# A graph sweep on one core: additions of counts without a wait for each other, and the loads of their places moved

## The chip, the cores and the metric

The kernel runs on 1 core of one Trainium2 chip. A core has a matrix engine (TensorE, PE in the profile; PEld is its loading of weights), a vector engine (VectorE, DVE), a scalar engine (ScalarE, ACT), GpSimd (POOL) and SyncE (SP). Each has an instruction queue of its own and waits for others by semaphores; SP, ACT and POOL also issue DMAs. The metric is the device time of one execution in microseconds (us): the median of 3 runs.

## The reference

A graph layer, batch norm and residual layer norm over N = 6250 nodes with D = 256 features and NE = 200000 edges, sorted by their target `dst`:

```
deg_out, deg_in = clip(segment_sum(1, src), 1), clip(segment_sum(1, dst), 1)
h = feats * rsqrt(deg_out)[:, None]
m = segment_sum(h[src], dst) * rsqrt(deg_in)[:, None]
x = m @ W_gc + b_gc + feats @ W_res + b_res
y = x + moe_ff(x)          # 64 experts, top 2, 256 -> 512 -> 256, gelu
out = layernorm(feats + batchnorm(y))
```

The targets are `6250 * u**2` with u uniform, so low nodes have many edges and high nodes few. The change lies in the stage that makes `segment_sum(h[src], dst)`, called the sweep here.

## The kernel before, in words

Ahead of the sweep (up to about 190 us) the degrees are counted and `h` is made, in SBUF (`hrow`) and in DRAM (`h_dram`). Behind it come routing, the experts and the two norms.

The edges stand in 1563 groups of 128 in order of their targets. The first 1118 groups are *dense*: for a window of 128 target nodes (a *column* c of 30), the kernel makes the matrix of counts (how many edges go from source s to window node t) and multiplies it with all of `hrow`. A column is cut into n *parts* of k groups, each part covering w neighbouring window nodes (`DENSE[c]` is g0, k, w, n). Part by part:

- DVE makes one-hots: `lo_of` (L684, through the helper at L287) the low digit of the source for 8 groups at a time, `hot_of` (L690) the high digit together with the target for a batch of groups.
- PE multiplies the two for each group (L712) into one of 5 PSUM banks `pc`: 49 x w counts in each of 128 partitions.
- ACT copies all but the part's first node to its place in `counts[c % 2]` (L729, L732), at a column that is read from a register.
- DVE adds the part's first node there (L749, 128 x 49), since that node can also be the last one of the part in front. The addition is made one part late (`carried`, L745). It frees the bank.

The places come from the table `places`: every eighth part a `TENSOR_LOAD` (L716) brings eight numbers into registers of ACT and DVE, at the point where the part's copy is written. Every addition was made to wait for the addition before it on the same engine, because two of them could touch the same column.

`multiply(c, t)` (L755) then takes the finished counts, 49 steps of two matmuls (L758, L759). The sweep's order is written out by hand in `dense` (L879): while column c is multiplied, column c + 1 is counted, so the additions of column 5 lie beside the multiplication of column 4. The remaining 445 groups are gathered: POOL fetches 128 rows of `h_dram` for one group by an indirect DMA (L626) into a ring of 8 blocks `r`, and PE multiplies each with a one-hot made on DVE (L631, L632, L935). These are put between the rest at equal distances of estimated time, and a block's next fetch is issued behind its last use. `x_step` puts small pieces of the next stage in between.

A check on the data (`off_parts`, L422, on the rises of nodes from part to part, given in `part`) sends everything to a slow general path when a part's nodes do not fit in its w.

Of the kernel before, what the change touches and what calls it, by code (L numbers as in the profile page):

```python
# [9 lines left out]
F32 = mybir.dt.float32  # L10
# [6 lines left out]
ALU = mybir.AluOpType  # L17
# [3 lines left out]
DVE_E = mybir.EngineType.DVE  # L21
SP_E = mybir.EngineType.SP
PE_E = mybir.EngineType.PE
ACT_E = mybir.EngineType.Activation

N = 6250
# [11 lines left out]
NE = 200000  # L38
NGR = 1568
NGU = -(-NE // 128)  # L40
WIN = 128
# [7 lines left out]
PAIRS = 8  # L49
# [36 lines left out]
def _node(g):  # L86

    return N * min(1.0, g * 128 / NE) ** 2
# [54 lines left out]
DENSE, GATHER, DENSE_PE = _plan()  # L143
GD = GATHER[0][0]
ND = len(DENSE)
# [6 lines left out]

BELOW = [max(0, int(_node(c[0]) - MARGIN) // TP) for c in DENSE]
ABOVE = [NT] + [-(-int(_node(c[0]) + WIN + MARGIN) // TP) for c in GATHER[:-1]]
LOW = [b * TP for b in BELOW] + [0] * len(GATHER)
# [4 lines left out]
def gnn_moe_kernel(ctx, tc, x_in, x_cols, src, dst, bases, nexts, firsts, parts, lasts, W_gc, b_gc, W_res, b_res, Wg, bg, w1, b1, w2, b2,  # L162
                   gamma, beta, out):
    nc = tc.nc
    V, S, G, T = nc.vector, nc.scalar, nc.gpsimd, nc.tensor
# [81 lines left out]
    with tc.tile_pool(name="edges", bufs=1) as ep, ExitStack() as later:  # L247
        iota_h = ep.tile([128, NS * WMAX, 2], FP16, name="iota_h")
        for a in range(0, NS * WMAX, 128):
            b = min(a + 128, NS * WMAX)  # L250
            V.tensor_scalar(iota_h[:, a:b, :], iota_f[:, :b - a, None].to_broadcast([128, b - a, 2]), float(a), None,
                            op0=ALU.add)
# [9 lines left out]
        places = ep.tile([ND, NPM], I32, name="places")  # L262
# [9 lines left out]
        for c, (g0, k, w, n) in enumerate(DENSE):  # L272
            a = g0
            while a < g0 + k * n:
# [4 lines left out]
                a = b  # L279
# [20 lines left out]
        with tc.tile_pool(name="late", bufs=1) as lp, tc.tile_pool(name="both", bufs=2) as bp, \  # L300
# [24 lines left out]
            part = dp.tile([128, 2, ND], F32, name="part")  # L325
# [19 lines left out]
            a, wides = 0, []  # L345
            for c, (g0, k, w, n) in enumerate(DENSE):
                if c == ND - 1 or DENSE[c + 1][2] != w:
# [3 lines left out]
                    a = c + 1  # L351
            S.activation(rows_w[:, 1, :], rows_w[:, 0, :], AF.Copy, scale=-1.0, bias=float(WIN - 1))
            pos = dp.tile([128, ND], F32, name="pos")
            away = dp.tile([128, 3, ND], F32, name="away")
# [8 lines left out]
            for k, values in enumerate((LOW, HIGH)):  # L363
                c = 0
# [36 lines left out]
            stepf = dp.tile([1, ND], F32, name="stepf")  # L401
            risen = dp.tile([ND, NPM], F32, name="risen")
            G.memset(stepf, 0.0)

            def windows():

# [14 lines left out]

            def off_parts():  # L422
                V.tensor_tensor(away[:, 0, :], part[:, 1, :], rows_w[:, 0, :], ALU.is_gt)
                V.tensor_scalar(away[:, 1, :], part[:, 1, :], 0.0, None, op0=ALU.is_lt)
                V.tensor_add(away[:, 0, :], away[:, 0, :], away[:, 1, :])

            def off_windows():
# [78 lines left out]
            for i in range(NGR // CG):  # L506
# [32 lines left out]
                for c in range(CG):  # L539
                    r = c % 2  # L540
# [3 lines left out]
                    else:  # L544
                        T.matmul(stp[64 * r:64 * r + 64, :], hot_row[:, c // 2, :, r], stairs[:, c - CV, :],
                                 start=(i == 0 and c < CV + 2), stop=(c0 + c >= NGR - 2))
# [13 lines left out]
                if i % 6 == 0 and 6 <= i <= 42:  # L560
                    r = i // 6 * 7
# [44 lines left out]
        with tc.tile_pool(name="xs", bufs=1) as xs, tc.tile_pool(name="hotg", bufs=2) as hg, \  # L606
# [12 lines left out]
            for i in range(NR):  # L619
                r = rp.tile([128, 2 * D + 2], F32R, name=f"r{i}")  # L620
# [25 lines left out]
            live = {"carry": []}  # L646
# [37 lines left out]
            def lo_of(q):  # L684

                if q * PAIRS < GD:
                    los[q] = hc.tile([128, PAIRS // 2, 128, 2], BF16, name="lo")
                    hot_pairs(los[q], lo_b, q * PAIRS, PAIRS, 128)

            def hot_of(q):  # L690
# [10 lines left out]
                for g in range(a, b):  # L701
                    hots[g] = hot[:, (g - e) // 2, :, (g - e) % 2]

            def count(g):

                c, j, i = groups[g]
                g0, k, w, n = DENSE[c]
                if i == 0:
                    live["pc"] = ps_c.tile([128, 512], F32, name="pc")
                r = g % PAIRS  # L710
                pc = live["pc"][:, :NS * w]
                T.matmul(pc, los[g // PAIRS][:, r // 2, :, r % 2], hots.pop(g), start=(i == 0),  # L712
                         stop=(i == k - 1))
                if i == k - 1:
                    if j % 8 == 0:
                        _, live["at"] = nc.values_load_multi_w_load_instructions(  # L716
                            places[c:c + 1, j:j + 8], engines=(ACT_E, DVE_E), min_val=0, max_val=WIN - w,
                            skip_runtime_bounds_check_because="clipped to what the window leaves")
                    carried(1)
                    at, pc = live["at"][j % 8], pc.rearrange("p (t w) -> p t w", w=w)  # L720
                    if j == 0:
                        live["adds"], live["carry"], live["puts"] = [], [], []
                    if c == 0 and j == 0:
                        live["puts"].append(S.copy(counts[0][:, :, :w], pc).ins)
                    else:
                        if j == 0:
                            step = nc.values_load(step_i[0:1, c:c + 1], engines=(DVE_E,), min_val=0, max_val=WIN - 1,
                                                  skip_runtime_bounds_check_because="clipped to the window")
                            put = S.copy(counts[c % 2][:, :, 1:w], pc[:, :, 1:])  # L729
                            to, had = counts[c % 2][:, :, 0:1], counts[(c - 1) % 2][:, :, ds(step, 1)]  # L730
                        else:
                            put = S.copy(counts[c % 2][:, :, 1:][:, :, ds(at, w - 1)], pc[:, :, 1:])  # L732
                            to = had = counts[c % 2][:, :, ds(at, 1)]
                        for a in live["adds"]:
                            tc.declare_no_dep(put.ins, a, reason="other columns of the window")
                        live["carry"].append((to, pc[:, :, 0:1], had, j))
                        live["puts"].append(put.ins)
                if g % PAIRS == 1:
                    lo_of(g // PAIRS + 1)
                if g == cuts[cut_of[g]][1] - 1:  # L740
                    hot_of(cut_of[g] + KB)
                if i == k - 1 and j == n - 1:
                    carried(0)

            def carried(but):  # L745

                while len(live["carry"]) > but:
                    to, more, had, j = live["carry"].pop(0)
                    add = V.tensor_tensor(to, more, f32(had), ALU.add).ins  # L749
                    tc.add_manual_dep(add, live["puts"][j].name, SYNCED, reason="its bank, and the column of the part in front")  # L750
                    for a in live["puts"][j + 1:]:
                        tc.declare_no_dep(add, a, reason="columns behind it")
                    live["adds"].append(add)

            def multiply(c, t):  # L755
# [212 lines left out]
            now, n = 0.0, 0  # L968
# [6 lines left out]
            for n in range(n, len(rows)):  # L975
# [6 lines left out]
                                    skip_runtime_bounds_check_because="a flag")  # L982
# [3 lines left out]
                                      skip_runtime_bounds_check_because="all groups or none")  # L986
            with tc.For_i(0, n_groups, 1) as gi:
# [10 lines left out]
                                       op0=ALU.mult, op1=ALU.add)  # L998
# [6 lines left out]
                for k in range(2):  # L1005
# [11 lines left out]
                start = ge.tile([128, 1], F32, name="start")  # L1017
                V.tensor_copy(start, low[:, 0:1])
                n_win = nc.values_load(numi, min_val=0, max_val=N // WIN + 1,
                                       skip_runtime_bounds_check_because="counted from the node numbers")  # L1020
                with tc.For_i(0, n_win, 1):
                    at = ge.tile([128, 1], F32, name="at")
# [45 lines left out]
    order = rpool.tile([1, E], I32, name="order")  # L1068
# [55 lines left out]
    with tc.tile_pool(name="xw", bufs=1) as xw, tc.tile_pool(name="xl", bufs=3) as xl, \  # L1124
# [42 lines left out]
        with tc.manual_schedule():  # L1167
            sums = {}
            for t0 in range(ta, tb, 2):
                n = min(2, tb - t0)  # L1170
# [9 lines left out]
            for t0, z in sums.items():  # L1180
                n = min(2, tb - t0)
# [4 lines left out]
                for t in range(t0, t0 + n):  # L1186
                    V.scalar_tensor_tensor(x[:, t, :], z[:, t - t0, :D], s_in[:, t - t0:t - t0 + 1], x[:, t, :],
                                           op0=ALU.mult, op1=ALU.add)
# [20 lines left out]
            for a, b in ((0, ta), (tb, NT)):  # L1209
                for t0 in range(a, b, 10):  # L1210
                    n = min(10, b - t0)
# [245 lines left out]
    with tc.tile_pool(name="ex", bufs=2) as xp, \  # L1457
# [202 lines left out]
        with tc.manual_schedule(engines={PE_E, ACT_E, DVE_E, SP_E}):  # L1660
# [6 lines left out]
                                skip_runtime_bounds_check_because="a flag")  # L1667
        with tc.For_i(0, n_left, 1), tc.tile_pool(name="all", bufs=1) as ap:
            V.memset(y_sum, 0.0)
            with tc.For_i(0, E, 1) as r:  # L1670
# [14 lines left out]
                with tc.For_i(0, FULL, 1) as i:  # L1685
                    idc = xp.tile([128, 1], I32, name="idc")
                    V.tensor_copy(idc, ids8[:, ds(i, 1)])
                    to = xp.tile([128, 1], I32, name="toc")
# [9 lines left out]
    with tc.tile_pool(name="fin", bufs=1) as fp, tc.tile_pool(name="gat", bufs=4) as gp, \  # L1698
# [71 lines left out]
        part = {}  # L1770
# [114 lines left out]
```

## Time and profile before

| | us |
|---|---|
| runs | 1501.49, 1506.61, 1509.82 (median 1506.61) |
| profiled execution | 1507.11 |
| its span | 1505.1 |
| granted TensorE clock, mean | 0.959 |
| sweep, first and last multiplication | about 190 to 905 |

In the profile a row of the engines' table is busy time, share and count of instructions. In rows of a group, "x" is the count, then come busy time, mean ns of one, the idle time of the engine ahead of them and what ended it. A row of waits has total us, times and the longest. A row of the timeline has start, duration, engine and line; "x2" means that two are merged, from the start of the first to the end of the second. Instructions of one engine overlap at their ends.

### The profile page before, as it was taken

What the parts mean: (1) busy time and instruction counts of PE and PEld (TensorE: products, weight loads), DVE (VectorE), ACT (ScalarE), POOL (GpSimd) and SP (SyncE); (2) the same over time, 40 slices, a digit from 0 to 9 for tenths busy, and PEclk for the clock granted to TensorE, in tenths of its full rate; (3) what the DMA queues carried; (4) which work ended last, traced back from release to release, by engine and by line L of the source; (5) the groups of instructions that cost most, each with busy time, mean ns of one, the idle gap of its engine ahead of it and who ended that gap; (6) DMA issues with size and microseconds to landing.
All of it is one profiled execution on the core that took longest, in us unless ns stands there. A gap on an engine that the chain in (4) does not pass through costs nothing. (4 is left out here: it accounts for less than half of the span.)

```text
span 1505.1 us, 33098 instructions
## 1 busy us (share of the span) xinstructions
PE 1347.8 (90%) x9805; PEld 1127.7 (75%) x9805; DVE 1127.2 (75%) x3325; ACT 763.2 (51%) x1966; POOL 797.9 (53%) x897
## 2 busy tenths in 40 slices
PE   5999478988999999999999994699999999999783
PEld 3555266877888899999999993588788888788441
DVE  8999889988888888888777746745555655444587
ACT  4676544456666666665555533433343333333358
POOL 6000215777776677776666635256666667565100
PEclk8999789999999999999999996899999999999888
DMA  5899665778777778787777755669777788687645
GB/s 180 264 283 323 240 241 155 197 220 236 201 221 221 220 214 232 210 221 211 222 203 217 214 156 192 125 196 295 229 247 253 253 251 268 206 250 246 236 142 155
DMA packets 211234, 332.81 MB, mean 221 GB/s; under 512 B 27989, under 2 KB 142814, under 8 KB 211045
## 3 DMA queue, kind: packets, MB, share of 16 engines
q1 hardware_dynamic: 156035, 176.48, 37.5%
q0 software_dynamic: 47888, 146.88, 34.4%
q10 hardware_dynamic: 7122, 7.26, 1.7%
q8 instruction: 79, 1.29, 0.4%
q14 instruction: 110, 0.90, 0.2%
HBM read 250.92 MB, written 73.15 MB: 215 GB/s over the span
## 5 line engine op out<-in xcount | busy, mean ns | idle before, releaser
L626 POOL DMA_INDIRECT r<-h_dram,srcg x445 | 469.8, 1056 | 243.3 <-PE pc L712 80.2
L758 PE MATMUL sm<-hrow,counts 128*128 128x258 f32 x1470 | 487.0, 346 | 8.8 <-DVE counts L749 8.7
L732 ACT CAST counts<-pc 128x196 f32 (+7 forms) x879 | 356.9, 406 | 211.1 <-PE pc L712 175.4
L759 PE MATMUL sm<-hrow,counts 128*128 128x256 f32 x1470 | 394.5, 282 | 0.0
L712 PE MATMUL pc<-hotk,lo 128*128 128x245 bf16 (+7 forms) x1118 | 304.7, 304 | 42.5 <-DVE counts L749 20.3
L758 PEld LDWEIGHTS sm<-hrow,counts 128*128 128x128 f32 x1470 | 286.6, 195 | 27.4 <-issue 12.4
L699 DVE TENSOR_TENSOR hotk<-key,iota_h 128x784 bf16<-128x784 f16 (+4 forms) x488 | 247.6, 507 | 57.9 <-PE pc L712 55.8
L759 PEld LDWEIGHTS sm<-hrow,counts 128*128 128x128 f32 x1470 | 279.8, 190 | 1.3
L749 DVE TENSOR_TENSOR counts<-pc,counts 128x49 f32 x908 | 218.6, 241 | 48.3 <-ACT counts L732 10.3
L1523 ACT ACTIVATE hT<-ph,bc 128x112 f32<-128x112 f32 (+16 forms) x256 | 108.4, 428 | 265.4 <-PE ph L1521 255.1
L1521 PE MATMUL ph<-xgT,w1s 128*128 128x112 f32 (+17 forms) x1024 | 198.7, 340 | 0.4 <-DVE xgT L1506 0.4
L1521 PEld LDWEIGHTS ph<-xgT,w1s 128*128 128x128 f32 x1024 | 166.0, 192 | 20.5 <-issue 2.2
L1481 POOL DMA_INDIRECT y_dram<-ys,dest x124 | 120.7, 973 | 106.5 <-ACT ys L1575 68.9
L712 PEld LDWEIGHTS <-lo 128*128 128x128 bf16 x1118 | 99.5, 100 | 74.9 <-issue 17.1
L631 PE MATMUL pg<-r,hot 128*128 128x258 f32 x445 | 144.5, 325 | 2.9 <-DMA r<-h_dram,srcg 2.4
L1481 POOL DMA_INDIRECT xg<-x_dram,ids x124 | 119.0, 959 | 49.8 <-issue 15.2
L632 PE MATMUL pg<-r,hot 128*128 128x256 f32 x445 | 125.1, 281 | 0.0
L1537 PE MATMUL py<-w2s,hT 128*128 128x256 f32 (+4 forms) x440 | 105.2, 382 | 0.0
L470 PE MATMUL pr<-wcat,f 128*128 128x512 f32 x196 | 100.8, 638 | 0.8 <-DMA wcat<-in_L_gnn_W_res_dram 0.8
L1506 DVE TENSOR_SCALAR xgT<-pte,bsum 128x112 f32<-128x112 f32 (+14 forms) x128 | 48.7, 421 | 67.2 <-PE pte L1503 67.0
L287 DVE TENSOR_TENSOR lo<-lo_b,iota 128x1024 bf16<-128x1024 bf16 x140 | 96.0, 686 | 3.3 <-issue 2.9
L1559 PE MATMUL ph<-hT,w2s 128*128 128x208 f32 (+8 forms) x464 | 95.0, 358 | 0.0
(361 smaller groups left out, 1965.8 us busy)
## 6 DMA issues: line engine op xcount, KB each, us to landing
w1s<-in_L_gnn_w_dram SPq DMA_DIRECT2D x64, 512.0 KB
w2s<-in_L_gnn_w_dram SPq DMA_DIRECT2D x64, 512.0 KB
y_dram<-zeros SPq DMA_DIRECT2D x48, 256.0 KB
yr<-y_dram SPq DMA_DIRECT2D x10, 1024.0 KB
h_dram<-hrow SPq DMA_DIRECT2D x5, 1536.0 KB
r<-h_dram,srcg POOLq DMA_INDIRECT x445
f<-in_x_cols_dram SPq DMA_DIRECT2D x25, 256.0 KB
z_dram<-zeros ACTq DMA_DIRECT2D x7, 903.0 KB
```

The costliest lines, as they stand in the source:

```text
L626: G.indirect_dma_start(out=f32(r[:, :2 * D]), out_offset=None, in_=h_dram[:, :], in_offset=bass.IndirectOffsetOnAxis(ap=idx, axis=0))
L631: T.matmul(pg, hot, r[:, D:], start=first, stop=False)
L632: T.matmul(pg[:, :D], hot, r[:, :D], start=False, stop=last)
L699: V.tensor_tensor(hot, pairs(key, e, n, m), iota_h[:, None, :m, :].to_broadcast([128, n // 2, m, 2]), ALU.is_equal)
L712: T.matmul(pc, los[g // PAIRS][:, r // 2, :, r % 2], hots.pop(g), start=(i == 0), stop=(i == k - 1))
L732: put = S.copy(counts[c % 2][:, :, 1:][:, :, ds(at, w - 1)], pc[:, :, 1:])
L749: add = V.tensor_tensor(to, more, f32(had), ALU.add).ins
L758: T.matmul(sm, by, hrow[:, t, D:], start=(t == 0), stop=False)
L759: T.matmul(sm[:, :D], by, hrow[:, t, :D], start=False, stop=(t == NS - 1))
L1481: w = G.indirect_dma_start(**kw)
L1521: T.matmul(ph[:, :m], w1s[:, kk, c * 128:(c + 1) * 128], xgT[:, kk, :m], start=(kk == 0), stop=(kk == 1))
L1523: S.activation(hT[:, c, :m], ph[:, :m], AF.Gelu, bias=b1_e[:, c:c + 1])
```

## The change

It does four things. The table `APART` says, from the expected density of edges, for which column c and which 32 parts the nodes at which parts start can be trusted to rise from each part to the next: for 817 of the 909 parts, which is none in columns 0 and 1, those from the 34th on in column 2, and all but the first in the others. For these, an addition is declared free of the additions before it (`declare_no_dep` in `carried`), and a `nop` is written between two that follow each other. The check asks for a rise of at least 1 in those parts (`least`), where it asked for 0. And the load of eight places is written where the low one-hots of the next 8 groups are made (`octet`), not at the part that uses them first.

```diff
--- before.py
+++ after.py
@@ -152,6 +152,13 @@
+def _apart(g, k):
+
+    d = NE / (2.0 * (N * max(_node(g), 0.5)) ** 0.5)
+    return d + 6.0 * d ** 0.5 < 128 * k
+
+
+APART = {(c, r): _apart(g0 + r * k, k) for c, (g0, k, w, n) in enumerate(DENSE) for r in range(0, 128, 32)}
 BELOW = [max(0, int(_node(c[0]) - MARGIN) // TP) for c in DENSE]
 ABOVE = [NT] + [-(-int(_node(c[0]) + WIN + MARGIN) // TP) for c in GATHER[:-1]]
 LOW = [b * TP for b in BELOW] + [0] * len(GATHER)
@@ -401,6 +408,13 @@
             stepf = dp.tile([1, ND], F32, name="stepf")
             risen = dp.tile([ND, NPM], F32, name="risen")
             G.memset(stepf, 0.0)
+            least = dp.tile([128, ND], F32, name="least")
+            for r in range(0, 128, 32):
+                some_c = [c for c in range(ND) if not APART[c, r]]
+                assert some_c == list(range(len(some_c)))
+                G.memset(least[r:r + 32, :], 1.0)
+                if some_c:
+                    G.memset(least[r:r + 32, :len(some_c)], 0.0)
             def windows():
@@ -421,7 +435,7 @@
             def off_parts():
                 V.tensor_tensor(away[:, 0, :], part[:, 1, :], rows_w[:, 0, :], ALU.is_gt)
-                V.tensor_scalar(away[:, 1, :], part[:, 1, :], 0.0, None, op0=ALU.is_lt)
+                V.tensor_tensor(away[:, 1, :], part[:, 1, :], least, ALU.is_lt)
                 V.tensor_add(away[:, 0, :], away[:, 0, :], away[:, 1, :])
             def off_windows():
@@ -701,6 +715,15 @@
                 for g in range(a, b):
                     hots[g] = hot[:, (g - e) // 2, :, (g - e) % 2]
+            octets = {DENSE[c][0] + j * DENSE[c][1]: (c, j) for c in range(ND) for j in range(0, DENSE[c][3], 8)}
+
+            def octet(g):
+
+                c, j = octets.pop(g)
+                live["at", c, j] = nc.values_load_multi_w_load_instructions(
+                    places[c:c + 1, j:j + 8], engines=(ACT_E, DVE_E), min_val=0, max_val=WIN - DENSE[c][2],
+                    skip_runtime_bounds_check_because="clipped to what the window leaves")[1]
+
             def count(g):
                 c, j, i = groups[g]
@@ -712,10 +735,10 @@
                 T.matmul(pc, los[g // PAIRS][:, r // 2, :, r % 2], hots.pop(g), start=(i == 0),
                          stop=(i == k - 1))
                 if i == k - 1:
+                    if g - k + 1 in octets:
+                        octet(g - k + 1)
                     if j % 8 == 0:
-                        _, live["at"] = nc.values_load_multi_w_load_instructions(
-                            places[c:c + 1, j:j + 8], engines=(ACT_E, DVE_E), min_val=0, max_val=WIN - w,
-                            skip_runtime_bounds_check_because="clipped to what the window leaves")
+                        live["at"] = live.pop(("at", c, j))
                     carried(1)
                     at, pc = live["at"][j % 8], pc.rearrange("p (t w) -> p t w", w=w)
                     if j == 0:
@@ -733,10 +756,13 @@
                             to = had = counts[c % 2][:, :, ds(at, 1)]
                         for a in live["adds"]:
                             tc.declare_no_dep(put.ins, a, reason="other columns of the window")
-                        live["carry"].append((to, pc[:, :, 0:1], had, j))
+                        live["carry"].append((to, pc[:, :, 0:1], had, j, j > 0 and APART[c, (j - 1) // 32 * 32]))
                         live["puts"].append(put.ins)
                 if g % PAIRS == 1:
                     lo_of(g // PAIRS + 1)
+                    for a in range(g + 1, g + PAIRS + 1):
+                        if a in octets:
+                            octet(a)
                 if g == cuts[cut_of[g]][1] - 1:
                     hot_of(cut_of[g] + KB)
                 if i == k - 1 and j == n - 1:
@@ -745,11 +771,17 @@
             def carried(but):
                 while len(live["carry"]) > but:
-                    to, more, had, j = live["carry"].pop(0)
+                    to, more, had, j, apart = live["carry"].pop(0)
+                    if apart and next(i for i in reversed(nc.cur_bb.bb.instructions)
+                                      if i.engine == live["adds"][-1].engine) is live["adds"][-1]:
+                        V.nop()
                     add = V.tensor_tensor(to, more, f32(had), ALU.add).ins
                     tc.add_manual_dep(add, live["puts"][j].name, SYNCED, reason="its bank, and the column of the part in front")
                     for a in live["puts"][j + 1:]:
                         tc.declare_no_dep(add, a, reason="columns behind it")
+                    if apart:
+                        for a in live["adds"]:
+                            tc.declare_no_dep(add, a, reason="runs start at nodes in rising order")
                     live["adds"].append(add)
             def multiply(c, t):
```

How this moves instructions shows on DVE while column 5 is counted. `ISA` sets the registers of the addition behind it, `places` is the load, `counts<-pc` an addition, in brackets stand the semaphores it waits for (DVE's own, ACT's, PE's). Before:

```order
L699 TENSOR_TENSOR hotk_5418<-key_92,iota_h_85 128x784 [waits PE_49]
L716 TENSOR_LOAD places_96
L749 ISA
L749 TENSOR_TENSOR counts1_2821<-pc_5405,counts1_2821 128x49 [waits DVE_49,Activation_49]
L749 ISA
L749 TENSOR_TENSOR counts1_2821<-pc_5414,counts1_2821 128x49 [waits DVE_49,Activation_49]
L287 TENSOR_TENSOR lo_5450<-lo_b_94,iota_2_73 128x1024
```

The same place after the change:

```order
L713 TENSOR_TENSOR hotk_5460<-key_92,iota_h_85 128x784 [waits PE_49]
L778 ISA
L778 TENSOR_TENSOR counts1_2827<-pc_5445,counts1_2827 128x49 [waits Activation_49]
L778 ISA
L778 TENSOR_TENSOR counts1_2827<-pc_5455,counts1_2827 128x49 [waits Activation_49]
L294 TENSOR_TENSOR lo_5475<-lo_b_94,iota_2_73 128x1024
L723 TENSOR_LOAD places_96
```

The load has moved from ahead of the two additions to behind the low one-hot, the wait for DVE's own work is gone, and nothing stands between the two additions (the `nop` leaves no row). Over the whole program 902 of the 908 additions wait for DVE before, and 87 after.

The second place is DVE in column 3, where parts have two groups. Before:

```order
L699 TENSOR_TENSOR hotk_4464<-key_92,iota_h_85 128x490 [waits PE_49]
L935 TENSOR_TENSOR hot_4466<-keyg_93,iota_f_71 128x512
L749 ISA
L749 TENSOR_TENSOR counts1_2821<-pc_4430,counts1_2821 128x49 [waits DVE_49,Activation_49]
L699 TENSOR_TENSOR hotk_4478<-key_92,iota_h_85 128x490 [waits PE_49]
```

After:

```order
L713 TENSOR_TENSOR hotk_4482<-key_92,iota_h_85 128x490 [waits DVE_49,PE_49]
L967 TENSOR_TENSOR hot_4484<-keyg_93,iota_f_71 128x512
L778 ISA
L778 TENSOR_TENSOR counts1_2827<-pc_4466,counts1_2827 128x49 [waits Activation_49]
L713 TENSOR_TENSOR hotk_4496<-key_92,iota_h_85 128x490 [waits DVE_49,PE_49]
```

Here the wait for DVE moved from the addition to the one-hots, for the earlier writer of their buffer. The order of the work on PE, POOL and SP is the same in both, but for five fills of `least` on POOL.

## The prediction

> **What bounds the kernel now.** I read the page first, then the busy table by stage, then who waits for whom inside the stage that the change touches, and last the engines' timelines there.
>
> ```profile
> span 1505.1 us, 33098 instructions
> PE 1347.8 (90%) x9805; PEld 1127.7 (75%) x9805; DVE 1127.2 (75%) x3325; ACT 763.2 (51%) x1966; POOL 797.9 (53%) x897
> ```
>
> The averages name TensorE (PE), but the sweep lies between about 190 and 905 us, and there the engines change places. Busy time by stretch (PE, PEld, DVE, ACT, POOL; then clock and DMA):
>
> ```profile
> 218.00:262.00 44.00, 34.76 (x267) 28.86 (x265) 39.69 (x123) 20.82 (x67) 26.82 (x26) 1.00 0.56 151
> 262.00:323.00 61.00, 56.70 (x440) 49.39 (x439) 56.10 (x177) 28.43 (x77) 47.90 (x44) 1.00 0.75 207
> 323.00:411.00 88.00, 79.01 (x604) 69.16 (x604) 77.08 (x289) 54.97 (x161) 64.91 (x63) 1.00 0.78 221
> 411.00:533.00 122.00, 116.03 (x898) 105.16 (x899) 106.18 (x381) 77.35 (x203) 86.38 (x82) 1.00 0.79 218
> 533.00:890.00 357.00, 356.58 (x2748) 336.07 (x2747) 284.16 (x940) 215.59 (x470) 243.82 (x232) 1.00 0.77 215
> ```
>
> From 533 on PE is busy 356.58 of 357 us: a faster VectorE (DVE) is worth nothing there. Before that PE is idle 9.2 us (218 to 262), 4.3 (262 to 323), 9.0 (323 to 411) and 6.0 us (411 to 533). What PE waited for, in the second, third and fourth of these stretches:
>
> ```profile
> PE pg L631 <- DMA r<-h_dram,srcg: 2.4, 3, 1.2
> PE pc L712 <- DVE counts L749: 1.5, 3, 0.8
> ...
> PE pc L712 <- DVE counts L749: 7.0, 19, 0.8
> PE sm L758 <- DVE counts L749: 1.0, 3, 0.4
> ...
> PE pc L712 <- DVE counts L749: 3.4, 8, 1.2
> PE sm L758 <- DVE counts L749: 2.7, 5, 0.7
> ```
>
> So from 323 to 533 the wait that ends last is for the additions of L749, which give a PSUM bank back. From 262 to 323 it is mostly for a gathered block `r`: another bound, which matters below.
>
> PE's idle time is understated, because matmul ends are modelled. In the saturated stretch these rows show the real pace:
>
> ```profile
> 700.27 0.28 PE L758 MATMUL sm<-hrow,counts 128*128 128x258 f32 x1
> 700.39 0.28 PE L759 MATMUL sm<-hrow,counts 128*128 128x256 f32 x1
> 700.51 0.35 PE L712 MATMUL pc<-hotk,lo 128*128 128x392 bf16 x1
> 700.55 0.43 PE L758 MATMUL sm<-hrow,counts 128*128 128x258 f32 x1
> 700.82 0.28 PE L759 MATMUL sm<-hrow,counts 128*128 128x256 f32 x1
> ```
>
> One large matmul every 0.12 us, and 0.31 for a counting one with a large one, so 0.19 for 392 columns. From 323 to 533 PE ran this:
>
> ```profile
> L758 PE MATMUL sm<-hrow,counts 128*128 128x258 f32 x393 | 133.7, 347 | 3.3 <-DVE counts L749 3.3
> L759 PE MATMUL sm<-hrow,counts 128*128 128x256 f32 x393 | 107.8, 280 | 0.0
> L712 PE MATMUL pc<-hotk,lo 128*128 128x294 bf16 (+2 forms) x331 | 93.6, 286 | 11.7 <-DVE counts L749 10.4
> L631 PE MATMUL pg<-r,hot 128*128 128x258 f32 x141 | 45.4, 322 | 0.0
> ```
>
> L632 follows each L631, so 1068 large ones x 0.12 = 128 us; 331 counting ones at 294 columns, 0.19 x 294/392 = 0.14 each, 47 us; some 100 small ones at 0.12, 12 us. That is 187 of 210 us: PE could gain up to 23 us between 323 and 533 (15.0 by the busy table).
>
> **The change part by part.** The main part takes the wait for DVE's own last addition from an addition (902 of 908 have it before, 87 after). What such a wait costs is seen where two additions stand side by side (start, then duration):
>
> ```profile
> 354.11 0.26 DVE L749 TENSOR_TENSOR counts<-pc,counts 128x49 fp32r<-128x49 f32 x1
> 354.26 0.41 DVE L699 TENSOR_TENSOR hotk<-key,iota_h 128x490 bf16<-128x490 f16 x1
> ...
> 357.45 0.41 DVE L699 TENSOR_TENSOR hotk<-key,iota_h 128x490 bf16<-128x490 f16 x1
> 357.78 0.59 DVE L749 TENSOR_TENSOR counts<-pc,counts 128x49 f32 x2
> 358.27 0.41 DVE L699 TENSOR_TENSOR hotk<-key,iota_h 128x490 bf16<-128x490 f16 x1
> ```
>
> An addition takes 0.24 to 0.26, but the instruction behind it starts 0.15 after its start (354.11 to 354.26) when it need not wait. A pair spans 0.59: the second starts 0.59 - 0.24 = 0.35 after the first. So a pair loses 0.35 - 0.15 = 0.20 us. Where a one-hot stands between two additions nothing is lost: its own 0.33 covers the wait. In the order, 123 freed additions of columns 5 to 12 stand right behind another: 57 in columns 5 to 7 (added between 323 and 411) and 66 in columns 8 to 12 (411 to 533). That is 11.4 + 13.2 = 24.6 us of DVE time, on an engine that is 88% and 87% busy there (77.08 of 88, 106.18 of 122). In columns 0, 1 and the first 33 parts of column 2 nothing changes; columns 3 and 4 have one pair each; from 533 on it is hidden by PE.
>
> The Trainium skill, "VectorE: DVE Perf Modes", section "The DRAIN you can't avoid", speaks against this: eight chained copies took the same time with a semaphore after each as with one at the end, "the semaphore costs nothing extra here". By it the term would be zero. The rows above disagree (0.15 against 0.35), and its section "Two Vector instructions with no wait between them" agrees with them, since by it the next instruction is held only at another start quadrant.
>
> The gain has to pass GpSimd (POOL), which issues the gathers that PE's fixed order takes in between. POOL from 255 to 345, its waits there, and POOL from 345 to 533:
>
> ```profile
> L626 POOL DMA_INDIRECT r<-h_dram,srcg x65 | 70.7, 1088 | 19.8 <-PE pc L712 8.8 <-issue 4.0 <-PE pg L632 4.0
> ...
> POOL r L626 <- PE pc L712: 8.8, 29, 0.3
> POOL r L626 <- issue: 4.0, 13, 0.3
> ...
> L626 POOL DMA_INDIRECT r<-h_dram,srcg x129 | 135.0, 1046 | 54.1 <-PE pc L712 29.5 <-PE sm L759 14.4 <-issue 5.8
> ```
>
> In the first, 65 x 0.305 = 19.8 us: each idle time is the least there is, so POOL is saturated at 1.09 + 0.305 = 1.39 us a gather, and PE catches up with it. Whatever DVE gains before 323 is lost there; I take 0 (ends: 0, and the 2.4 us of 12 freed pairs in column 2). After it the least is 1.046 + 0.305 = 1.351 us. How far POOL is ahead, by the counts up to 320, 411 and 533:
>
> ```profile
> L626 POOL DMA_INDIRECT r<-h_dram,srcg x66 | 72.6, 1099 | 72.7 <-DMA h_dram<-hrow 43.7 <-PE pg L632 13.8 <-PE pc L712 7.0
> L631 PE MATMUL pg<-r,hot 128*128 128x258 f32 x63 | 21.5, 341 | 2.8 <-DMA r<-h_dram,srcg 2.4 <-ACT counts L732 0.3 <-issue 0.2
> ...
> L631 PE MATMUL pg<-r,hot 128*128 128x258 f32 x124 | 40.9, 330 | 2.8 <-DMA r<-h_dram,srcg 2.4 <-ACT counts L732 0.3 <-issue 0.2
> ...
> L626 POOL DMA_INDIRECT r<-h_dram,srcg x213 | 226.0, 1061 | 132.3 <-DMA h_dram<-hrow 43.7 <-PE pc L712 39.9 <-PE pg L632 18.2
> L631 PE MATMUL pg<-r,hot 128*128 128x258 f32 x206 | 67.6, 328 | 2.9 <-DMA r<-h_dram,srcg 2.4 <-ACT counts L732 0.3 <-issue 0.2
> ```
>
> It is 3 ahead when PE waits for it, 7 at the end. If PE stays at 3 ahead, the 61 gathers to 411 need 82.4 of 91 us (8.6 to gain) and the 82 to 533 need 110.8 of 122 (11.2 more). So each stretch has three caps: DVE 11.4, POOL 8.6, PE 9.0 by the table, then DVE 13.2, POOL 11.2, PE 6.0 by the table (together PE up to 23 by pace). The smallest are 8.6 and 6.0, 14.6 together; by pace the second rises to 11.2, 19.8 together. Since an engine that just stops being the bound still makes the others wait now and then, I take 8 and 5.
>
> The second part moves the load of eight places on DVE and ACT behind a low one-hot.
>
> ```profile
> L716 DVEq TENSOR_LOAD <-places x127: 593/609/2017, 170.8 to 884.5; - x127
> ```
> ```profile
> DVE counts L749 <- ACT counts L732: 5.2, 14, 0.5
> ...
> DVE counts L749 <- DVE hotk L699: 1.1, 4, 0.3
> ```
>
> The load takes DVE's sequencer 0.61 us. Ahead of an addition it is covered by one hotk (0.33); behind the low one-hot it gets a cover of that operation's size. Visible between 323 and 533 are the 1.1 us in which an addition started late behind a hotk, and at most the 5.2 us of waiting for ACT, whose load only moves to another place between two copies. So 0 to 6 us of DVE time; I take 1, under caps that already bind.
>
> The new `least` is five small GpSimd fills in a stage where POOL is nearly idle, and one comparison against a tile in place of one against a number: 0, at most a few tenths. Waits come back elsewhere: 88 one-hots, all but a few in columns 2 to 4, and 29 small operations of x_step in columns 5 to 12 now wait for DVE where an addition did it for them. A one-hot waits for the writer of its buffer, which is four batches old (two for the low ones), long done: 0, and the last rival prices the other end. The 29 cost 0.20 each at worst, 5.8 us; I take 1, which eats the load's gain. PE, SP and the DMAs keep their order.
>
> Sum: 8 + 5 = 13 us off the profiled 1505.1, whose run took 1507.11, close to the median of 1506.61. So 1506.6 - 13 = 1493.6.
>
> **The rivals.** Half a per cent, 7.5 us, is about what a measurement of this kernel can tell from no change.
>
> *All of DVE's loss comes back.* If the gathers can follow with fewer than 3 blocks ahead, or POOL's fetches get shorter, the caps are DVE's 24.6 and PE's 23 us: 1506.6 - 23 = 1483.6. For it speaks that PE waited for a gather for only 2.4 us in the stretch where POOL is saturated. Against it, POOL has shown nothing below 0.305 us of idle time there, and the 23 us would need it to issue 143 gathers in 187 us, 1.31 each.
>
> *Nothing reaches the end.* Either a second addition is not taken earlier although it need not wait (a DVE that finishes each operation first, as the page's rule has it), or PE's waits only change their name, from L749 to the gathered `r`. Then the time is 1506.6, at most 3 us less for the parts between. For it speaks the stretch from 262 to 323, where PE's main wait is a gather already; against it the 0.15 us spacing, and POOL's 54.1 us idle for 129 fetches after 345, where the least would be 39.3.
>
> *Slower: the waits move onto the one-hots.* In columns 2 to 4, some 85 one-hots get a wait of their own. If it held DVE until its latest operation had ended, each would pay the pair's 0.20 us: 17 us between 220 and 323, where DVE is 90 to 92% busy and the change gives nearly nothing back. With the 13 us gained later this ends at 1506.6 + 17 - 13 = 1511; with little gained, at 1524. It decides when the waited operation is the one just in front; the buffers' ages speak against that.
>
> **How the numbers follow.** The partial gain, from 5 to 18 us: 0.60. All of it, 18 to 25 us: 0.12. Nothing, within 5 us either way: 0.22. Slower by the moved waits: 0.06. The prediction is the likeliest case's 1493.6. The range goes up to 1504, into the case of no effect, and down to 1484, the whole loss; beyond it lie the slower case and half of the no-effect case, 0.17 in all. The partial case gains more than 7.5 us with about 0.58 of its 0.60, since its smallest caps already make 14.6 us and the discount on them would have to be half; with the whole recovery that is 0.70 for faster, 0.25 for the same, 0.05 for slower.
>
> **What would show it.** In the timeline from 323 to 411, two additions side by side span about 0.38 to 0.40 instead of 0.59. PE's waits for the counts of the additions fall from 7.0 and 3.4 us to under half, and waits for `r` reach into this stretch. POOL's longest idle times there fall towards 0.3. The stretch from 533 on keeps its length, and the last multiplication of the sweep comes 10 to 16 us earlier; everything behind it moves as a block. Wrong in the first step: pairs still span 0.5 or more. Wrong in the second: pairs shrink, PE's waits for DVE fall, and the end of the sweep stays, with POOL at 0.305 throughout. Wrong the other way: POOL fetches take less than 1.0 us on the mean once DVE is less crowded, and the gain passes 18 us.

## The result and the profile after

The changed kernel takes 1492.32 us (median of 6 runs, 1490.54 to 1494.24) against 1506.98 us for the kernel before beside it (6 runs, 1501.49 to 1509.82): a ratio of 0.990, interval 0.989 to 0.992. The profiled execution took 1492.21 us. The head of its page:

```profile
span 1490.1 us, 32393 instructions
PE 1344.2 (90%) x9805; PEld 1125.9 (76%) x9805; DVE 1107.1 (74%) x3325; ACT 760.2 (51%) x1966; POOL 801.0 (54%) x902
```

DVE does the same 3325 instructions in 20 us less busy time (neighbouring additions now overlap, and an overlap counts once). The last multiplication of the sweep, in the timelines before and after:

```profile
905.10 0.28 PE L759 MATMUL sm<-hrow,counts 128*128 128x256 f32 x1
```
```profile
891.89 0.28 PE L791 MATMUL sm<-hrow,counts 128*128 128x256 f32 x1
```

So 13.2 us of the span's 15.0 come out of the sweep. The other 1.8 lie behind it. Of ten variants profiled below whose later stages can be compared, nine also have a shorter rest than this profile of before (by 0.2 to 3.8 us), among them three that leave the additions as they were; so I do not count the 1.8 as the change's.

The busy table by stage (PE, PEld, DVE, ACT, POOL; then clock and DMA):

```profile
262.00:323.00 61.00, 55.26 (x405) 46.74 (x404) 53.91 (x170) 26.59 (x71) 47.74 (x44) 0.97 0.73 208
323.00:411.00 88.00, 83.92 (x667) 74.25 (x665) 79.59 (x312) 59.33 (x176) 68.50 (x65) 1.00 0.80 225
411.00:533.00 122.00, 119.06 (x932) 109.37 (x932) 105.06 (x390) 79.88 (x208) 94.87 (x90) 0.99 0.82 234
533.00:876.00 343.00, 343.00 (x2650) 324.27 (x2649) 261.92 (x906) 206.91 (x451) 230.05 (x224) 1.00 0.78 216
```

From 323 to 411 PE gets through 667 matmuls instead of 604, from 411 to 533 through 932 instead of 898. Behind that it is busy throughout, as before. The clock column, 1.00 in all these stretches before, now reads 0.97 and 0.99 in two of them: for 3.4 us each, from 277.7 and from 414.2, the granted clock is 0.50, both times next to a wait of PE for a gathered block (1.3 and 1.4 us). This is not what limits the gain: in `adds_5_12` below the clock is 1.00 in all these stretches, and the sweep is shorter by nearly as much. What PE waited for from 262 to 533, first before, then after:

```profile
PE pc L712 <- DVE counts L749: 11.9, 30, 1.2
PE sm L758 <- DVE counts L749: 4.1, 8, 0.8
PE pg L631 <- DMA r<-h_dram,srcg: 2.4, 3, 1.2
```
```profile
PE pg L645 <- DMA r<-h_dram,srcg: 11.0, 19, 1.4
PE sm L790 <- DVE counts L778: 0.4, 1, 0.4
PE pg L645 <- ACT resg L990: 0.3, 1, 0.3
PE pc L735 <- DVE counts L778: 0.2, 1, 0.2
```

The waits for additions are gone, 16.0 us to 0.6; the waits for a gathered block have grown from 2.4 to 11.0. By these waits the bound has passed from DVE to the fetches that POOL issues; the experiments test it. The start of each column's multiplication, after minus before, is read from the two timelines: column 2 starts 3.9 us earlier, column 4 (323 us) 0.1 later, column 7 (411 us) 7.4 earlier, column 12 (533 us) 11.8, column 16 and all behind it 13.0 to 13.2. The whole gain lies between columns 4 and 16.

DVE's timeline shows the cause at its smallest:

```profile
352.54 0.39 DVE L778 TENSOR_TENSOR counts<-pc,counts 128x49 f32 x2
352.83 0.41 DVE L713 TENSOR_TENSOR hotk<-key,iota_h 128x490 bf16<-128x490 f16 x1
353.15 0.39 DVE L778 TENSOR_TENSOR counts<-pc,counts 128x49 f32 x2
```

A pair spans 0.39 us instead of 0.59. From 240 us on the second of two neighbouring additions starts 0.147 us after the first (median of 270 neighbours), before the change 0.343.

POOL, in the groups from 262 to 520 after the change, and its idle time there by what ended it (only the three largest):

```profile
L640 POOL DMA_INDIRECT r<-h_dram,srcg x187 | 201.6, 1078 | 57.0 <-PE pc L735 24.1 <-issue 10.7 <-PE sm L791 8.5
```
```profile
POOL r L640 <- PE pc L735: 24.1, 79, 0.3
POOL r L640 <- issue: 10.7, 35, 0.3
POOL r L640 <- PE sm L791: 8.5, 28, 0.3
```

57.0 us over 187 fetches is 0.305 each, the least there is: POOL has no slack from 262 to 520. The same group before:

```profile
L626 POOL DMA_INDIRECT r<-h_dram,srcg x180 | 191.3, 1063 | 67.6 <-PE pc L712 34.9 <-PE sm L759 14.1 <-issue 8.8
```

There 67.6 us stood against a least of 180 x 0.305 = 54.9. The timelines say the same in another way. After the change each of these 187 blocks had been free (its last matmul, at L646, had ended) for at least 2.4 us, 4.9 at the median, when POOL came to issue its next fetch. Before, 58 of 179 were refilled within 0.5 us of becoming free, 1.1 at the median. So after the change POOL does not wait for room in the ring; the ring waits for POOL.

### The profile page after: what moved, and what is told of

It reads as the page before. It is cut to its first block, busy times and chain, and to the rows that moved or that the text cites. A ratio compares the mean times of both kernels' runs of the same rounds, so it can differ in the third digit from the quotient of the medians.

```text
span 1490.1 us, 32393 instructions
## 1 busy us (share of the span) xinstructions
PE 1344.2 (90%) x9805; PEld 1125.9 (76%) x9805; DVE 1107.1 (74%) x3325; ACT 760.2 (51%) x1966; POOL 801.0 (54%) x902
## 5 line engine op out<-in xcount | busy, mean ns | idle before, releaser
L778 DVE TENSOR_TENSOR counts<-pc,counts 128x49 f32 x908 | 194.1, 238 | 9.3 <-ACT counts L755 3.8
L645 PE MATMUL pg<-r,hot 128*128 128x258 f32 x445 | 146.4, 329 | 11.8 <-DMA r<-h_dram,srcg 11.0
L646 PE MATMUL pg<-r,hot 128*128 128x256 f32 x445 | 125.7, 283 | 0.0
L645 PEld LDWEIGHTS pg<-r,hot 128*128 128x128 f32 x445 | 86.2, 194 | 19.5 <-DMA r<-h_dram,srcg 16.9
```

The costliest lines, as they stand in the source:

```text
L645: T.matmul(pg, hot, r[:, D:], start=first, stop=False)
L646: T.matmul(pg[:, :D], hot, r[:, :D], start=False, stop=last)
```

## Experiments

The theory: freeing the additions gives DVE back the pairs' 0.20 us, about 25 us in columns 5 to 12, and POOL's rate of gathers lets 13 of it through. Rivals: the place loads made the gain; PE's own pace is the cap; the gain comes from freed additions elsewhere.

### One part alone

`adds_only` frees the additions and loads the places where they were loaded before:

```diff
                 if i == k - 1:
-                    if g - k + 1 in octets:
-                        octet(g - k + 1)
                     if j % 8 == 0:
+                        octet(g - k + 1)
                         live["at"] = live.pop(("at", c, j))
...
                     lo_of(g // PAIRS + 1)
-                    for a in range(g + 1, g + PAIRS + 1):
-                        if a in octets:
-                            octet(a)
```

> The additions freed as in the change, the loads of the places left where they stood before. Theory (the pairs of additions give the DVE time, and the gathers' issue on POOL caps it): 11 to 15 us faster than before, about 1493 to 1495, pairs spaced 0.15 us. Rival (the loads matter as much): 5 to 8 us faster, about 1500.

`loads_only` moves the loads and leaves the waits on the additions:

```diff
-                        live["carry"].append((to, pc[:, :, 0:1], had, j, j > 0 and APART[c, (j - 1) // 32 * 32]))
+                        live["carry"].append((to, pc[:, :, 0:1], had, j, False))
```

> The loads of the places moved behind the low one-hots, every addition still waiting for the one before it. Theory: 0 to 2 us faster than before, about 1505 to 1507, pairs still spaced 0.34 us. Rival (the loads matter as much): 5 to 8 us faster, about 1500.

Measured beside 1506.46 us: the freed additions alone 1491.39, ratio 0.990 (0.989 to 0.992), the sweep 12.3 us shorter; the loads alone 1502.51, ratio 0.998 (0.9973 to 0.9995), the sweep 3.9 us shorter, which is more than the 0 to 2 us expected. The last multiplication of the sweep in each:

```profile
892.83 0.28 PE L787 MATMUL sm<-hrow,counts 128*128 128x256 f32 x1
```
```profile
901.18 0.28 PE L791 MATMUL sm<-hrow,counts 128*128 128x256 f32 x1
```

PE's waits from 262 to 533 with the additions alone:

```profile
PE pg L645 <- DMA r<-h_dram,srcg: 9.1, 17, 1.5
PE pc L735 <- DVE counts L774: 1.7, 6, 0.5
```

and with the loads alone:

```profile
PE pc L735 <- DVE counts L778: 10.6, 23, 1.2
PE pg L645 <- DMA r<-h_dram,srcg: 4.2, 5, 1.4
PE sm L790 <- DVE counts L778: 3.2, 4, 1.4
```

The freed additions make the change. The loads give 2 to 4 us by themselves (2.4 by the ratio). On top of the additions they give nothing that the times show (0.990 with and without them), and 0.9 us in the sweep of one profile each (12.3 against 13.2). So the two do not add up, as would be so under a common cap.

### With half of the fetches

`after_half` and `before_half` leave out every second refill of the ring of gathered blocks; PE multiplies whatever lies in the block:

```diff
-                if n + NR < len(rows):
+                if n + NR < len(rows) and n % 2 == 0:
                     fetch(ring[n % NR], srcg[:, rows[n + NR][1] - GD:rows[n + NR][1] - GD + 1])
```

> The changed kernel with every second fetch of the ring left out (PE multiplies what the block held before, so that the sums are not the reference's). POOL then issues about half the gathers, and less is moved. Theory (after the change the issue rate of the gathers is what PE waits for from 262 to 520 us): PE's waits for r vanish, and the time falls by 8 to 14 us more than the changed kernel, to 1478 to 1484. Rival (the rest of PE's idle time comes from DVE and ACT as they hand banks over, not from POOL): within 3 us of the changed kernel, 1489 to 1493.

> The kernel before with every second fetch of the ring left out (sums not the reference's). Theory (before the change DVE's additions are the bound from 323 to 533 us and POOL from 262 to 323 alone): 2 to 6 us faster than before, 1501 to 1505. Rival (POOL was the bound all along): 10 us or more faster.

The expected totals were missed by far: 11557 and 11590 us. The sums of the sweep feed the routing behind it, and with these sums the experts had far more to do. The largest group of the changed kernel's run from 1500 to 11000 us:

```profile
L1553 PE MATMUL ph<-xgT,w1s 128*128 128x128 f32 x7728 | 1740.8, 416 | 214.4 <-DVE xgT L1538 214.4
```

The totals say nothing on the change; the sweep lies ahead of the routing and can be read. Its last multiplication, in before and in after with half of the fetches:

```profile
900.36 0.28 PE L759 MATMUL sm<-hrow,counts 128*128 128x256 f32 x1
```
```profile
875.05 0.28 PE L791 MATMUL sm<-hrow,counts 128*128 128x256 f32 x1
```

With gathers that can follow, the change is worth 900.36 - 875.05 = 25.3 us instead of 13.2, of which 4.1 fall ahead of column 4 and 21.2 behind its start. Without the change, halving the fetches gives 4.7, as expected; with it 16.8, above the 8 to 14 expected. PE's waits from 262 to 533, before and after with half of the fetches:

```profile
PE pc L712 <- DVE counts L749: 11.7, 30, 1.2
PE sm L758 <- DVE counts L749: 3.4, 7, 0.7
```
```profile
PE pc L735 <- DVE counts L778: 2.1, 6, 0.8
PE sm L790 <- DVE counts L778: 0.4, 1, 0.4
```

No wait for a block is left in either. So the cap on the change lies with the fetches, not with PE. Half of the fetches is also half of their traffic; this pair does not tell POOL's issue from the landing of the data.

### More room for the fetches

Two edits give POOL more time without fewer fetches: a ring of 10 blocks, and gathers that begin at 62 instead of 76 us of the planner's time.

```diff
-            NR = 8
+            NR = 10
```

> The changed kernel with a ring of 10 gathered blocks in place of 8. POOL sat idle for 9.5 us ahead of the first gather's multiplication, because the ring was full. Theory (POOL's issue rate is what PE waits for from 262 to 520 us): two more fetches leave in that idle time, so POOL is 2 x 1.36 = 2.7 us further on for the whole stretch; 1 to 3 us faster than the changed kernel, 1489 to 1491, and PE's waits for r fall. Rival (the ring's depth and not POOL's rate makes PE wait): POOL's idle times at the 0.305 floor disappear and 5 us or more are gained. Rival (PE's idle time left is DVE's): no change, 1491 to 1493.

```diff
-LEAD = 76.0
+LEAD = 62.0
```

> The changed kernel with the first gather put 14 us of estimated time earlier in PE's order (LEAD 62 in place of 76) and all later ones a little further apart. Theory (POOL's rate): POOL loses its 9.5 us of idle time at the start, and the demand moves ahead by less and less, 7.5 us at the 200th gather; 3 to 7 us faster than the changed kernel, 1485 to 1489. Rival (DVE is the bound again at that place): no change or slower, 1492 to 1496, with PE waiting for additions between 218 and 262.

Measured beside 1504.21 us: the ring 1488.32, ratio 0.989 (0.987 to 0.991), the sweep 2.5 us shorter than the changed kernel's; the lead 1485.65, ratio 0.987 (0.986 to 0.989), 2.9 shorter. By the ratios the ring gives 1.8 us and the lead 4.5 over the changed kernel (0.989 to 0.992). The ring's interval overlaps with that one widely, so its gain rests on the sweep of one profile; the lead's hardly touches it. POOL from 262 to 520 with the ring of 10:

```profile
L640 POOL DMA_INDIRECT r<-h_dram,srcg x188 | 203.1, 1080 | 57.3 <-PE pc L735 20.5 <-PE sm L791 11.3 <-DMA r<-h_dram,srcg 11.0
```

It remains at 0.305 us of idle time a fetch: two more blocks add two fetches' worth of head start and no rate. The early lead takes away an idle time ahead of 262. POOL's waits for the last use of a block (L646) from 218 to 262, in the changed kernel and with the early lead:

```profile
POOL r L640 <- PE pg L646: 10.1, 3, 9.5
```
```profile
POOL r L640 <- PE pg L646: 2.1, 7, 0.3
```

In the changed kernel POOL stands 9.5 us with a full ring before its saturated stretch begins. Starting earlier uses those 9.5 us, at the price of a column 3 that starts 5.3 us later than in before; the sweep still ends 16.1 us earlier than there.

### Later gathers

The gathers are put at equal distances of estimated time. `after_spread` moves them later, by up to ten distances in the middle; `before_spread` does the same to the kernel before:

```diff
-                while n < len(rows) and now > LEAD + n * every:
+                while n < len(rows) and now > LEAD + (n + 10.0 * min(n / 200, (len(rows) - n) / 245)) * every:
```

> The changed kernel with the gathers spread otherwise in PE's order: up to the 200th each stands 5% further apart, so that the 200th comes 10 places later, and the rest 4% closer. Theory (POOL's rate caps the stretch from 262 to 520 us, and POOL has room behind it): the cap there is loosened by about 10 x 1.36 = 13 us, PE's waits for r fall to under 3 us in all; 4 to 9 us faster than the changed kernel, 1483 to 1488. Rival (DVE or ACT take over at once): within 2 us of the changed kernel, with PE waiting for additions in place of r.

> The same spread of the gathers in the kernel before. Theory (before the change DVE's additions are the bound from 323 to 533 us and POOL only from 262 to 323): 0 to 4 us faster than before, 1502 to 1507. Rival (POOL's rate was as much the bound before): as much gained as in the changed kernel, 4 to 9 us, 1498 to 1502.

Both missed: 1490.42, ratio 0.990 (0.988 to 0.992), and 1510.15, ratio 1.003 (1.002 to 1.005). In the first, column 16 starts 19.9 us earlier than in before, and then 6 us are lost ahead of the last column, column 29. Two waits there, one of DVE's from 840 to 905 us and the only one of PE from 860 to 890:

```profile
DVE xr L827 <- DMA xr<-r_dram: 4.1, 1, 4.1
```
```profile
PE sm L837 <- DVE xr L827: 2.1, 1, 2.1
```

The gathered windows now end late, and the kernel takes up a piece of the next stage only behind the windows whose sums it needs. By PE's timelines one such piece (4 matmuls at L837, 8 at L846), which lay beside column 27 in the changed kernel, has slid to column 28, which now holds two. Column 27 takes 19.4 us instead of 20.7, and column 28 takes 26.0 instead of 20.3. PE waits 2.1 us for that piece's input, which had only just been loaded, and from 870.7 to 874.1, behind this wait, the granted clock is 0.50. In the kernel before the same loss (7.5 us at the last column) meets no gain. `after_spread2` lets the delay run out at gather 380:

```diff
-                while n < len(rows) and now > LEAD + n * every:
+                while n < len(rows) and now > LEAD + (n + 10.0 * max(min(n / 200, (380 - n) / 180), 0.0)) * every:
```

> The changed kernel with the first 200 gathers 5% further apart in PE's order, and the lag of ten places made up by the 380th, not at the very end. Theory (POOL's issue rate caps the stretch from 262 to 520 us; the first spread lost 6 us again because the last windows came too late for the small pieces of the next stage): 5 to 8 us faster than the changed kernel, 1484 to 1487, with the multiplication of column 16 some 20 us earlier than before and that lead kept to the end of the sweep. Rival (the loss at the end comes from the closer gathers themselves): 1489 to 1493.

It took 1487.14 us beside 1504.45, ratio 0.988 (0.986 to 0.990). Column 28 holds one piece again and takes 20.3 us. Column 16 starts 19.0 us earlier than in before, and 17.2 of them are left at the end of the sweep. By the ratios this is 3.3 us better than the changed kernel where 5 to 8 were expected, and the intervals overlap. With a ring of 10 as well, and the same two edits in the kernel before:

> The same spread, and a ring of 10 blocks. Theory: the two reliefs of POOL's cap add up to PE's remaining idle time at most; 0 to 3 us faster than the spread alone, 1482 to 1487. Rival (the spread alone lifts the cap): the same as the spread alone.

> The same spread and ring of 10 in the kernel before, where additions wait for one another. Theory (DVE's additions are the bound there from 323 to 533 us): 0 to 4 us faster than before. Rival (POOL's rate was the bound before, too): 8 us or more faster.

1484.84, ratio 0.986 (0.985 to 0.988), the best of all and faster than both kernels; and 1503.85, ratio 0.999 (0.998 to 1.001). PE's waits from 262 to 533, in this form of the changed kernel and of the one before:

```profile
PE pg L645 <- DMA r<-h_dram,srcg: 6.2, 7, 2.0
PE pc L735 <- DVE counts L778: 2.1, 6, 0.5
```
```profile
PE pc L712 <- DVE counts L749: 12.7, 31, 1.3
PE sm L758 <- DVE counts L749: 2.8, 7, 0.8
PE pg L631 <- DMA r<-h_dram,srcg: 0.7, 3, 0.3
```

The same relief for POOL is worth about 6 us by the ratios (0.990 to 0.986; 6.8 in the sweep) where additions are free, and nothing that can be told from zero by the time (2.9 us in the sweep) where they are not: the order of the two bounds, seen from the other side.

### Where the freed additions count

`adds_5_12` frees only those of columns 5 to 12:

```diff
-                        live["carry"].append((to, pc[:, :, 0:1], had, j, j > 0 and APART[c, (j - 1) // 32 * 32]))
+                        live["carry"].append((to, pc[:, :, 0:1], had, j, j > 0 and 5 <= c <= 12 and APART[c, (j - 1) // 32 * 32]))
```

> The changed kernel with additions freed in columns 5 to 12 alone; in all other columns an addition still waits for the one before it. Theory (only there DVE's time is on the path and is not taken back by POOL): the changed kernel's time within 2.5 us, 1490 to 1495. Rival (the freed additions of columns 13 to 29 and of column 2 give a part): 4 us or more slower than the changed kernel.

1493.52 us beside 1504.45, ratio 0.993 (0.991 to 0.994); the sweep ends 12.8 us earlier, against 13.2. By the ratios it is 3.5 us slower than the changed kernel, between the 2.5 of the theory and the 4 of the rival, but the intervals overlap, and the profile of the sweep speaks for the theory. Behind column 12 pairs are again as before the change, as DVE's timeline shows:

```profile
600.16 0.59 DVE L778 TENSOR_TENSOR counts<-pc,counts 128x49 f32 x2
```

From column 12 to the end of the sweep this costs about 1 us: the lead over the kernel before grows by 1.4 us there in the changed kernel and by 0.3 here. PE is the bound there nearly throughout.

## Why the prediction came out

The forecast was 1493.6 us, the median is 1492.32: 13 us forecast, 14.7 by the medians, 13.2 of it in the sweep.

**The pair's 0.20 us.** Right: 0.343 to 0.147 us, 0.196 each. With the loads alone the neighbours stay 0.342 apart, with the additions alone they are 0.1475 apart: it is the wait. The Trainium skill, "VectorE: DVE Perf Modes", section "The DRAIN you can't avoid", has a semaphore cost nothing extra, measured there between copies; the trace disagrees, with 0.20 us for additions of 49 columns, and so do the 12.3 us of the additions alone.

**24.6 us of DVE time.** Right as counted: in the trace of before 57 pairs stand between 323 and 411 us and 66 between 411 and 533, and 123 x 0.196 = 24.1. With half of the fetches 21.2 us come back behind the start of column 4, and 4.1 ahead of it, where 2.4 were counted. The 21.2 are no measure of DVE's term alone, since PE is then busy 121.53 of the 122 us from 411 to 533. The place is right too: in the sweep, freeing columns 5 to 12 alone gives 12.8 of 13.2 us.

**POOL as the cap.** The mechanism was right, the discount's reason was not. The caps were 8.6 + 11.2 = 19.8 us for POOL and 9.0 + 6.0 for PE's table, and I took 8 + 5 from the smaller of each because an engine that just stops being the bound would still make others wait now and then. The stretches gave 7.5 us (323 to 411) and 5.6 (411 to column 16), close to 8 and 5, but POOL had no such moments: it was saturated from 262 to 520, and its own caps were lower than counted. Counts after the change, up to 320 and up to 520:

```profile
L640 POOL DMA_INDIRECT r<-h_dram,srcg x67 | 74.1, 1106 | 73.0 <-DMA h_dram<-hrow 43.7 <-PE pg L646 12.3 <-issue 8.8
L645 PE MATMUL pg<-r,hot 128*128 128x258 f32 x63 | 22.0, 349 | 6.0 <-DMA r<-h_dram,srcg 5.6 <-issue 0.2 <-DVE hotk L713 0.2
...
L640 POOL DMA_INDIRECT r<-h_dram,srcg x212 | 229.4, 1082 | 117.2 <-DMA h_dram<-hrow 43.7 <-PE pc L735 25.6 <-PE pg L646 18.7
L645 PE MATMUL pg<-r,hot 128*128 128x258 f32 x206 | 69.5, 337 | 11.8 <-DMA r<-h_dram,srcg 11.0 <-ACT resg L990 0.3 <-issue 0.2
```

145 fetches were issued and 143 taken in these 200 us. From the busy times, (229.4 - 74.1) / 145 = 1.071, and with 0.305 it is 1.376 us a fetch: 145 x 1.376 = 199.5 us, all there is. The forecast had 143 x 1.351 = 193.2 us. So the two mis-sized terms of POOL's cap are the fetch, 0.025 us longer than in the trace of before (3.6 us in all), and two more fetches ahead (2.7 us): 6.3 of the 6.8 us between the cap of 19.8 and the 13.0 measured. That sum holds for this trace. The longer fetch is not shown to come from the change: counted in the same way from 320 to 520, a fetch took 1.057 us with the additions alone and 1.041 with the early lead.

**PE's cap by the table, 9.0 + 6.0.** Wrong as a cap. With half of the fetches the change gives 10.7 us from column 4 to column 7 and 10.3 from there to column 16, and 21.2 in all, within the 23 by PE's real pace and not within the 15.0 of the busy table. The second term of the sum, 5, was a discount on this 6.0. The smallest cap that held there was POOL's, counted as 11.2, and that in turn was about twice the 5.6 that came. The two errors met, so that the second term came out right is luck, and with it the closeness of the total; the first, 8 for POOL's 8.6, came out at 7.5 with less of it.

**Nothing before 323.** Right: column 2 starts 3.9 us earlier and column 4 0.1 later, and PE's waits for `r` stand there: 5.6 us up to 320 in the counts above, where before they were 2.4.

**The loads, 1 us, cancelled by 1 for x_step's 29 waits.** Not contradicted: with the additions freed, the sweep is 13.2 us shorter with the loads moved and 12.3 without, and the times show no difference. Alone they gave 2.4 us by the ratio and 3.9 in the sweep, within the 0 to 6. The 29 waits were not tried by themselves.

**The waits moved onto one-hots, 0, and the slower rival.** The rival did not come: with half of the fetches columns 2 to 4 gained 4.1 us, where it would have cost 17. Taking those waits away again (the run with columns 5 to 12 alone) moved the end of the sweep by 0.4 us, to later.

**All of it comes back.** This rival, with 1483.6 us, needed fetches that can follow. It is what the sweep did when half of them were left out, and the ring with the later gathers goes most of that way by itself: 20.0 us off the sweep, 1484.84.

What stays open: why a fetch took 1.071 us in this trace, and whether POOL's 1.08 us of busy time for a fetch is its own work or hangs on the traffic. POOL's idle time at its least, in the changed kernel and with the ring of 10, and blocks that stand free for 2.4 us or more before their refill speak for POOL's issue; no run took the data's share away alone.

## What to carry to other kernels

When a wait is removed from a saturated engine, price what comes back, and then ask how much of it the next producer in the same fixed order can follow: here 25 us were freed and the gathers let 13 through. An engine whose every idle time is the least there is has no slack, however low its busy share; give it a head start (a deeper ring, an earlier begin, work due later) along with the change, since alone such room is worth little, as the runs of the kernel before showed. And when work is made due later, look at who reads its result last.

## What the runs showed of the hardware

A wait for DVE's own latest result costs a short operation of DVE 0.20 us (0.343 against 0.147 us between the starts of two additions of 49 columns), by kernels that differ in that wait and the `nop` that stands in its place. POOL issues indirect fetches of 128 rows back to back at 1.38 us each, 0.305 of it shown as idle, with a ring of 8 and of 10; and a stretch can be bound by it at a busy share of 78% (68.50 of 88 us). A longer wait of PE also goes together with a lower clock. In the sweeps of all these profiles, from column 1 on, PE had eight waits of 1.74 to 2.49 us, and next to each the granted clock was 0.50 for 3.4 us, as it was from 870.7 to 874.1 in `after_spread`. Of 26 waits of 1.0 to 1.6 us three had this next to them. No run tried what sets the length.
